# The scan stage of a hybrid vision block rebuilt: operands broadcast by DMA, decays in PSUM, products on GpSimd, directions added by an accumulating DMA

## The chip, the cores and the metric

The kernel runs on one core of a Trainium2 chip. The metric is the time of one execution in device microseconds (us), taken as the median of the runs shown; lower is better. A core has five engines with queues of their own: TensorE (PE in the profile, its weight loads PEld), VectorE (DVE), ScalarE (ACT), GpSimd (POOL) and SyncE (SP, which only issues DMAs here). Each engine works through its instructions in a fixed order. Where one waits, all that stand behind it on that engine wait too.

## The reference: what is computed

Four images of 64 x 64 tokens with 96 channels pass through a group norm and four layers. Layer 0 is a selective scan block over 192 inner channels, and it alone is changed:

```python
xz = x @ W_in.T
xp, z = xz[..., :192], xz[..., 192:]
xc = silu(conv3x3(xp) + conv_b)                  # u
xs = [xc by rows, xc by columns, and both reversed]   # four directions
dts, Bs, Cs = split(xs @ x_proj_w.T, [6, 16, 16])
delta = softplus(dts @ dt_proj_w.T + dt_proj_b)
# for each channel d (192) and state n (16), over the 4096 tokens t of a direction:
#   h[d, n] = exp(delta[t, d] * A[d, n]) * h[d, n] + delta[t, d] * u[t, d] * B[t, n]
#   y[t, d] = sum over n of h[d, n] * C[t, n]
y = sum of the four directions, each turned back to rows, + 4 * D * u
out = (y * silu(z)) @ W_out.T
```

The layers after it (a separable convolution, linear attention, two quantised feed-forward blocks and a spectral filter) are the same in both kernels.

## The kernel before, in words

`layer0` works on one image at a time, and `layers123` follows once all four images are through it. For image b, `pre(b)` makes, in eight blocks of 512 tokens, the gate `sz`, the convolved input `u`, the rows of B and C (`bc_s`), `delta_s` and `du_s` = delta times u; all of them go to DRAM. The scans then run over 24 groups (`NG`) of 8 channels: 8 channels x 16 states fill the 128 partitions. `post(b)` adds 4 D u, applies the gate, multiplies by `w_out` and stores x1.

For one group, `decay` (lines 237 to 255) loads 8 rows of delta and spreads each over its 16 states with a matmul against a 0/1 matrix `sel` (L248, tile `pa`). ScalarE then takes the exponential into `dA` (L252), 128 x 4096. `scan_group` (lines 257 to 322) spreads 8 rows of delta u in the same way (L275, `pb`), and VectorE multiplies them by the replicated B, `brep`, into `dB` (L279). ScalarE copies `dA` and `dB` into the column order (`dAT`, `dBT`, L281). Then VectorE runs four scans of 4096 steps: rows forward into `S` (L286), rows backward in place in `dB` (L287), columns forward into `T` (L294), columns backward in place in `dBT` (L295). It adds the two of each pair (L290, L298), adds the column sum to the row sum through a strided view (L299), and multiplies by the replicated C, `crep` (L307). TensorE sums the 16 states of each channel with the matrix `red` (L312, tile `py`), ScalarE copies the result out (L315), and SP stores it into `y_s` (L317).

`beside()` is called in the middle of a group. It gives out the next pieces of `post(b-1)` and `pre(b+1)`, and the `decay` of the next group. The tile framework's scheduler decides how these stand on each engine's queue. GpSimd issues stores in this stage and computes nothing in it. SP issues the loads and the stores of y. Before the first scan, `pre(0)` runs alone; after the last, `post(3)`. The lines named by the prediction are L236 (GpSimd's store of x1), L160, L179, L188, L207 (its other stores), L330 (the load of `brep`, one DMA for each 16 partitions), L491 and L666 (loads of the later layers) and L627 (a GpSimd memset there).

Of the kernel before, what the change touches and what calls it, by code (L numbers as in the profile page):

```python
# [10 lines left out]
F32 = mybir.dt.float32  # L11
# [7 lines left out]
NB = 4  # images  # L19
HW = 64  # rows, and columns, of an image  # L20
L = HW * HW  # tokens of an image
C = 96  # channels
DI = 192  # inner channels of the scan, and hidden ones of the spectral filter
NS = 16  # states of a scanned channel
NG = DI // 8  # groups of 8 scanned channels: 8 channels x 16 states on the partitions
RK = 6
BLK = 512  # tokens of one matmul: 8 image rows
# [3 lines left out]
N1 = 64  # the transform over 4096 tokens is 64 x 64  # L31


def conv_taps():
    """The 3x3 taps (ky, kx), the middle one first: it alone reaches every output."""
    return [(1, 1)] + [(y, x) for y in range(3) for x in range(3) if (y, x) != (1, 1)]


def tap_window(ky, kx, r0):
    """Rows (of the block's, from r0) and columns of the output that a tap reaches."""  # L40
    dy, dx = ky - 1, kx - 1
    ra, rb = max(0, -dy - r0), min(RPB, HW - dy - r0)
    ca, cb = max(0, -dx), min(HW, HW - dx)
    return dy, dx, ra, rb, ca, cb


@with_exitstack
def layer0(ctx: ExitStack, tc: tile.TileContext, a: dict, x1):
    """Group norm, the 2D selective scan block, the residual; x1[b] = relu(x + block), as the
    next layer reads it."""  # L50
# [20 lines left out]
    sel = const("sel", [40, 128], a["sel"])  # L71
# [3 lines left out]
    # Each of the four scans adds D u.  # L75
# [7 lines left out]
    delta_s = dram("delta_s", [DI, L])  # L83
    du_s = dram("du_s", [DI, L])
    bc_s = dram("bc_s", [2 * NS, L])
    u_s = dram("u_s", [DI, L])
    sz_s = dram("sz_s", [DI, L])
    y_s = dram("y_s", [DI, L])

    def halves(t):  # L90
        return t.rearrange("(c p) l -> p c l", p=C)
# [4 lines left out]
    def k4(name, shape=(C, 2, BLK)):  # L96
        return wk.tile(list(shape), F32, tag="k4", name=name, bufs=4)

    def pre_psum(name, rows=C, cols=BLK):
        t = ps.tile([128, BLK], F32, tag="pre", name=name, bufs=2)  # L100
        return t[:rows, :cols]

    def pre(b):
        """Everything before the scan, in blocks of 8 image rows."""
# [9 lines left out]
        # A group's three channels: its mean, and the mean of variance + squared distance of means.  # L114
# [15 lines left out]
        for i in range(NBLK):  # L130
# [4 lines left out]
            xb = k2("xb", (C, RPB + 2, HW))  # L135
# [3 lines left out]
            xn = k2("xn", (C, RPB + 2, HW))  # L139
            nc.scalar.activation(  # L140
                xn[:, :n, :], xb[:, :n, :], AF.Identity, scale=gn[:, 0:1], bias=gn[:, 1:2]
            )
            xp = k4("xp", (C, 2, RPB + 2, HW))
            for c in range(2):
                for ra, rb in ((0, 5), (5, n)):
                    p = pre_psum("p_xp", C, (rb - ra) * HW)
                    nc.tensor.matmul(
                        p, lhsT=w_in[:, c * C : (c + 1) * C], rhs=xn[:, ra:rb, :],
# [3 lines left out]
            sz = k4("sz")  # L152
            for c in range(2):
                p = pre_psum("p_z")
                nc.tensor.matmul(
                    p, lhsT=w_in[:, DI + c * C : DI + (c + 1) * C],
                    rhs=xn[:, r0 - lo : r0 - lo + RPB, :], start=True, stop=True,
                )
                nc.scalar.activation(sz[:, c, :], p, AF.Silu)  # L159
            nc.gpsimd.dma_start(halves(sz_s[b])[:, :, cols], sz)  # L160
            yield
            u = k4("u")
# [16 lines left out]
            nc.gpsimd.dma_start(halves(u_s[b])[:, :, cols], u)  # L179
# [8 lines left out]
            nc.gpsimd.dma_start(bc_s[b][:, cols], xd[RK : RK + 2 * NS, :])  # L188
            for c in range(2):
# [3 lines left out]
                # softplus(v) = max(v, 0) + log(1 + e), e = exp(-|v|); with w = fl(1 + e), the  # L193
                # logarithm is log(w) - ((w - 1) - e).
# [12 lines left out]
                nc.gpsimd.dma_start(delta_s[b][rows, cols], r)  # L207
                du = k2("du")
                nc.vector.tensor_tensor(du, r, u[:, c, :], ALU.mult)
                nc.gpsimd.dma_start(du_s[b][rows, cols], du)  # L210
            yield

    def post(b):
        """D u, the gate, the output projection and the residual."""
        for i in range(NBLK):
            cols = slice(i * BLK, (i + 1) * BLK)
            y, u, sz = k4("y_in"), k4("u_in"), k4("sz_in")
            nc.sync.dma_start(y, halves(y_s[b])[:, :, cols])
            nc.sync.dma_start(u, halves(u_s[b])[:, :, cols])
            nc.sync.dma_start(sz, halves(sz_s[b])[:, :, cols])  # L220
            xr = k2("xr")
            nc.sync.dma_start(xr, a["xT"][:, b * L + i * BLK : b * L + (i + 1) * BLK])
            p = pre_psum("p_out")
            for c in range(2):
                nc.vector.scalar_tensor_tensor(
                    y[:, c, :], u[:, c, :], d4[:, c : c + 1], y[:, c, :], ALU.mult, ALU.add
                )
            nc.vector.tensor_tensor(y, y, sz, ALU.mult)
            for c in range(2):
                nc.tensor.matmul(  # L230
                    p, lhsT=w_out[:, c, :], rhs=y[:, c, :], start=(c == 0), stop=(c == 1)
                )
            o = k2("o")
            nc.vector.tensor_tensor(o, p, xr, ALU.add)
            nc.scalar.activation(o, o, AF.Relu)
            nc.gpsimd.dma_start(x1[b][:, cols], o)  # L236
            yield

    def decay(b, g):
        """exp(delta A) of a group, [(channel, state), token]."""  # L240
        rows = slice(g * 8, (g + 1) * 8)
        dA = big.tile([128, L], F32, tag="dA", name="dA", bufs=2)
        for q in range(NBLK):
            if q % 2 == 0:
                dl = wk.tile([8, 2 * BLK], F32, tag="dl", name="dl", bufs=2)
                nc.sync.dma_start(dl, delta_s[b][rows, q * BLK : (q + 2) * BLK])
            pa = ps.tile([128, BLK], F32, tag="pa", name="pa", bufs=2)
            nc.tensor.matmul(  # L248
                pa, lhsT=sel[0:8, :], rhs=dl[:, (q % 2) * BLK : (q % 2 + 1) * BLK],
                start=True, stop=True,  # L250
            )
            nc.scalar.activation(  # L252
                dA[:, q * BLK : (q + 1) * BLK], pa, AF.Exp, scale=nega[:, g : g + 1]
            )
        return dA

    def scan_group(b, g, dA, brep, crep, beside):
        """The four scans of a group: by rows and by columns, each in both directions. They share
        their decays and inputs, and C is applied to the sum of their states."""
        rows = slice(g * 8, (g + 1) * 8)  # L260
        by_col = "p (w h) -> p h w"
        dAT = big.tile([128, L], F32, tag="dAT", name="dAT")
        dB = big.tile([128, L], F32, tag="dB", name="dB")
        dBT = big.tile([128, L], F32, tag="dBT", name="dBT")
        # The scans wait for these; the convolution beside them can come later.
        with tc.high_priority(offset=400):
            for q in range(NBLK):
                cols = slice(q * BLK, (q + 1) * BLK)
                hs = slice(q * RPB, (q + 1) * RPB)
                if q % 2 == 0:  # L270
                    # In another row group of the tensor engine than delta.
# [566 lines left out]
```

## Time and profile before

| | us |
|---|---|
| median of the 2 runs shown (9795.03 to 9818.39) | 9806.71 |
| span of the profiled execution, first to last instruction | 9822.7 |
| from the start to the load that precedes the first scan group | 482 |
| scans of the four images | 1742, 1736, 1785, 1667 |
| last `post` and `layers123` | some 2411 |
| VectorE busy in the whole span | 6735.3 |
| TensorE busy in the whole span | 6680.7 |
| ScalarE busy in the whole span | 3202.3 |
| GpSimd busy in the whole span | 159.9 |

The span is that of one profiled execution, and every duration below comes from it; it lies 16 us over the median. A row such as "L286 DVE TENSOR_TENSOR_SCAN S<-dA,dB 128x4096 ... x96 | 834.4, 8692" is read as: line 286, on VectorE, writes S from dA and dB, 96 times, 834.4 us in all and 8692 ns each. What stands behind the next bar is the idle time ahead of such instructions on their engine, and which instruction ended it.

### The profile page before, as it was taken

How to read it: one execution, taken by the hardware profiler on the slowest of the kernel's cores; microseconds unless marked ns; L12 is line 12 of the kernel's file. 1: busy time of each engine (PE TensorE's matmuls, PEld its weight loads, DVE VectorE, ACT ScalarE, POOL GpSimd, SP SyncE). 2: the span in 40 equal slices, each digit the busy share in tenths (PEclk: the TensorE clock that was granted, in tenths of full speed). 3: DMA queues.
4: the chain of work that ended last, by engine and by line, in shares of the span. 5: the costliest groups of instructions: out<-in, count | busy, mean ns of one | idle time of the engine just before them, and what ended most of it. 6: DMA issues, size and time to landing. Idle time of an engine off the chain costs nothing.

```text
span 9822.7 us, 58304 instructions
## 1 busy us (share of the span) xinstructions
PE 6680.7 (68%) x22202; PEld 3031.3 (31%) x22202; DVE 6735.3 (69%) x3526; ACT 3202.3 (33%) x4081; POOL 159.9 (2%) x296
## 2 busy tenths in 40 slices
PE   6767777754567666555666665554445888989888
PEld 2222222211122222111222211111112766848576
DVE  1188888887888888788988879989993323132232
ACT  3333434342334444333444433333330111121111
POOL 0000000000000000000000000000000000000000
PEclk8855565555566666555656655555556867777776
DMA  1110000002100000210000021000002010100000
GB/s 44 43 25 16 15 13 15 14 20 52 30 15 16 19 17 17 52 39 12 16 18 16 22 44 33 13 6 6 6 5 71 4 36 1 33 7 14 26 1 26
DMA packets 94661, 216.09 MB, mean 22 GB/s; under 512 B 25274, under 2 KB 26958, under 8 KB 92494
## 3 DMA queue, kind: packets, MB, share of 16 engines
q1 hardware_dynamic: 75950, 153.62, 6.4%
q0 software_dynamic: 18432, 58.74, 2.1%
q8 instruction: 177, 2.90, 0.1%
q14 instruction: 102, 0.84, 0.0%
HBM read 134.67 MB, written 77.59 MB: 22 GB/s over the span
## 4 chain that ended last, share of the span: by engine, by line
DVE 42%; PE 39%; ACT 8%; issue 8%; DMA 2%; SPq 0%; POOL 0%; DVEq 0%; ACTq 0%; POOLq 0%
DVE dB L287 8%; DVE T L294 8%; DVE dBT L295 6%; PE pb L275 6%; DVE S L286 6%; PE p_conv L169 5%; DVE S L290 4%; ACT dBT L281 4%; PE pa L248 4%; PE py L312 3%; PE p_l L499 3%; DVE S L299 2%; PE p_dft L653 2%; PE p_h L639 2%; ACT dAT L281 2%
## 5 line engine op out<-in xcount | busy, mean ns | idle before, releaser
L275 PE MATMUL pb<-du_g,sel 8*128 8x512 f32 x1536 | 1309.9, 1022 | 1517.7 <-DVE dB L279 1517.7
L248 PE MATMUL pa<-dl,sel 8*128 8x512 f32 x1536 | 1359.6, 1030 | 879.2 <-ACT dA L252 784.7
L281 ACT COPY dAT<-dA 128x512 f32<-128x512 f32 x768 | 772.3, 1104 | 2020.5 <-DVE dBT L295 2014.5
L286 DVE TENSOR_TENSOR_SCAN S<-dA,dB 128x4096 f32<-128x4096 f32 x96 | 834.4, 8692 | 576.2 <-PE py L312 494.2
L169 PE MATMUL p_conv<-xp,conv_w 96*96 96x504 f32 (+3 forms) x2304 | 1204.7, 684 | 2.8 <-ACT sz L159 2.8
L275 PEld LDWEIGHTS pb<-du_g,sel 8*128 8x128 f32 x1536 | 447.7, 307 | 2317.7 <-DVE dB L279 1843.4
L248 PEld LDWEIGHTS pa<-dl,sel 8*128 8x128 f32 x1536 | 411.2, 296 | 1762.8 <-ACT dA L252 1082.3
L287 DVE TENSOR_TENSOR_SCAN dB<-dA,dB 128x4096 f32<-128x4096 f32 x96 | 833.9, 8686 | 5.6 <-DVE S L286 0.5
L294 DVE TENSOR_TENSOR_SCAN T<-dAT,dBT 128x4096 f32<-128x4096 f32 x96 | 833.4, 8681 | 0.0
L295 DVE TENSOR_TENSOR_SCAN dBT<-dAT,dBT 128x4096 f32<-128x4096 f32 x96 | 833.2, 8679 | 0.1
L281 ACT COPY dBT<-dB 128x512 f32<-128x512 f32 x768 | 771.8, 1094 | 130.9 <-DVE T L298 80.8
L252 ACT ACTIVATE dA<-pa,nega 128x512 f32<-128x512 f32 x768 | 513.8, 685 | 715.2 <-PE pa L248 671.4
L299 DVE TENSOR_TENSOR S<-S,T 128x4096 f32<-128x4096 f32 x96 | 716.2, 7460 | 1.1
L169 PEld LDWEIGHTS p_conv<-xp,conv_w 96*96 96x96 f32 x2304 | 423.0, 190 | 802.8 <-issue 779.2
L279 DVE TENSOR_TENSOR dB<-pb,brep 128x512 f32<-128x512 f32 x768 | 492.9, 679 | 251.5 <-PE pb L275 201.8
L312 PE MATMUL py<-S,red 128*32 128x512 f32 x1536 | 401.7, 955 | 201.2 <-DVE S L307 177.3
L307 DVE TENSOR_TENSOR S<-S,crep 128x1024 f32<-128x1024 f32 x384 | 445.8, 1220 | 1.9
L290 DVE TENSOR_TENSOR S<-S,dB 128x4096 f32<-128x4096 f32 x96 | 424.4, 4421 | 2.0
L298 DVE TENSOR_TENSOR T<-T,dBT 128x4096 f32<-128x4096 f32 x96 | 423.9, 4416 | 0.3
L201 DVE TENSOR_SCALAR w<-e 96x512 f32<-96x512 f32 x64 | 26.3, 411 | 391.1 <-ACT e L199 391.1
L499 PE MATMUL p_l<-x,taps 96*96 96x504 f32 (+3 forms) x576 | 249.8, 597 | 29.8 <-DMA x<-x 29.8
L376 DVE COPY o<-p_o 128x192 f32<-128x192 f32 x64 | 22.9, 357 | 318.4 <-ACT o L372 318.4
(183 smaller groups left out, 6638.2 us busy)
## 6 DMA issues: line engine op xcount, KB each, us to landing
tw<-in_dft SPq DMA_DIRECT2D x32, 512.0 KB
sz_s<-sz POOLq DMA_DIRECT2D x32, 384.0 KB, 3.4
u_s<-u POOLq DMA_DIRECT2D x32, 384.0 KB, 3.4
delta_s<-r POOLq DMA_DIRECT2D x64, 192.0 KB, 2.4
du_s<-du POOLq DMA_DIRECT2D x64, 192.0 KB, 2.4
dl<-delta_s SPq DMA_DIRECT2D x384, 32.0 KB
du_g<-du_s SPq DMA_DIRECT2D x384, 32.0 KB
y_s<-ys SPq DMA_DIRECT2D x768, 16.0 KB
```

The lines of the kernel that those rows point to most:

```text
L169: nc.tensor.matmul(p[:, ra:rb, ca:cb], lhsT=conv_w[:, kc, ky * 3 + kx, oc * C : (oc + 1) * C], rhs=xp[:, kc, at + ra : at + rb, ca + dx : ...
L248: nc.tensor.matmul(pa, lhsT=sel[0:8, :], rhs=dl[:, (q % 2) * BLK : (q % 2 + 1) * BLK], start=True, stop=True,)
L275: nc.tensor.matmul(pb, lhsT=sel[32:40, :], rhs=du[32:40, (q % 2) * BLK : (q % 2 + 1) * BLK], start=True, stop=True,)
L281: nc.scalar.copy(dst.rearrange("p (w h) -> p w h", h=HW)[:, :, hs], src[:, cols].rearrange("p (h w) -> p w h", w=HW),)
L286: nc.vector.tensor_tensor_scan(S, dA, dB, 0.0, ALU.mult, ALU.add)
L287: nc.vector.tensor_tensor_scan(dB[:, ::-1], dA[:, ::-1], dB[:, ::-1], 0.0, ALU.mult, ALU.add)
L290: nc.vector.tensor_tensor(S, S, dB, ALU.add)
L294: nc.vector.tensor_tensor_scan(T, dAT, dBT, 0.0, ALU.mult, ALU.add)
L295: nc.vector.tensor_tensor_scan(dBT[:, ::-1], dAT[:, ::-1], dBT[:, ::-1], 0.0, ALU.mult, ALU.add)
L299: nc.vector.tensor_tensor(S.rearrange("p (h w) -> p h w", w=HW), S.rearrange("p (h w) -> p h w", w=HW), T.rearrange(by_col, h=HW), ALU.add,)
L312: nc.tensor.matmul(py[k : k + 32, :], lhsT=red, rhs=S[:, cols], start=True, stop=True)
L499: nc.tensor.matmul(p3[:, ra:rb, ca:cb], lhsT=taps[:, ky * 3 + kx, :], rhs=x3[:, r0 + dy + ra : r0 + dy + rb, ca + dx : cb + dx], start=(k ...
```

## The change

The row pair and the column pair of a group become two separate phases (b, g, o), o = 0 for rows and 1 for columns: 4 x 24 x 2 = 192 phases. A phase works in four steps q of 1024 tokens (`CH`).

- The partitions are ordered (state, channel), so one DMA can repeat 8 rows of delta, and of delta u, over all 128 partitions (`load`). No matmul spreads them.
- ScalarE takes the exponential from the loaded delta into PSUM (`decay`, tile `pa`, 128 x 1024, two buffers), once for the forward scan and once more for the backward one.
- GpSimd multiplies delta u by the replicated B (`inputs`) and the states by the replicated C.
- VectorE only scans, in steps of 1024: four forward, then four backward, each starting from the last column of the one before.
- The backward states are added to the forward ones by a DMA that accumulates, which GpSimd issues.
- The column order is made ahead in DRAM: `turn` loads a 96 x 4096 array, ScalarE copies it turned, and it is stored again, for B and C, delta, delta u, and for y of the columns in `post`.
- The stores of `pre` and `post` move from GpSimd's queue to SP's; work tiles have fewer buffers (`xp` one, `turn` and `turned` one).

Core of the diff (what is left out of `scan` and of the main loop is the same in kind):

```diff
+    def turn(src, dst):
+        n = src.shape[0]
+        t = wk.tile([C, L], F32, tag="turn", name="turn")
+        nc.sync.dma_start(t[:n, :], src)
+        for q in range(NCH):
+            o = wk.tile([C, CH], F32, tag="turned", name="turned")
+            w = CH // HW
+            nc.scalar.copy(
+                o[:n, :].rearrange("p (w h) -> p w h", h=HW),
+                t[:n, :].rearrange("p (h w) -> p w h", w=HW)[:, q * w : (q + 1) * w, :],
+            )
+            nc.sync.dma_start(dst[:, q * CH : (q + 1) * CH], o[:n, :])
...
+    def load(b, g, o):
+        rows = slice(g * 8, (g + 1) * 8)
+        dl, du = [], []
+        for q in range(NCH):
+            for dst, src, n, tag, bufs in ((dl, delta_s, "dl", "dl", 5), (du, du_s, "B", "B", 6)):
+                t = big.tile([128, CH], F32, tag=tag, name=n, bufs=bufs)
+                nc.sync.dma_start(
+                    t, src[o][b][rows, chunk(q)].unsqueeze(0).broadcast_to([NS, 8, CH])
+                )
+                dst.append(t)
+        return dl, du
+
+    def inputs(b, g, o, du):
+        for q in range(NCH):
+            nc.gpsimd.tensor_tensor(du[q], du[q], reps[o, 0][:, chunk(q)], ALU.mult)
+
+    def decay(g, dl, q):
+        pa = ps.tile([128, CH], F32, tag="pa", name="pa", bufs=2)
+        nc.scalar.activation(pa, dl[q], AF.Exp, scale=nega[:, g : g + 1])
+        return pa
+
+    def scan(b, g, o, dl, B, beside):
+        ...
+        for q in range(NCH):
+            pa = decay(g, dl, q)
+            s = big.tile([128, CH], F32, tag="S", name="S", bufs=6)
+            nc.vector.tensor_tensor_scan(
+                s, pa, B[q], S[-1][:, CH - 1 : CH] if S else 0.0, ALU.mult, ALU.add
+            )
+            S.append(s)
+        beside()
+        last = None
+        for q in reversed(range(NCH)):
+            pa = decay(g, dl, q)
+            nc.vector.tensor_tensor_scan(
+                B[q][:, ::-1], pa[:, ::-1], B[q][:, ::-1],
+                last[:, 0:1] if last is not None else 0.0, ALU.mult, ALU.add,
+            )
+            last = B[q]
+            nc.gpsimd.dma_start(S[q], B[q], accum_op=ALU.add)
+            nc.gpsimd.tensor_tensor(S[q], S[q], reps[o, 1][:, chunk(q)], ALU.mult)
+            if q % 2 == 1:
+                py = ps.tile([128, BLK], F32, tag="py", name="py")
+            for k in range(2):
+                at = 32 * (2 * (q % 2) + k)
+                nc.tensor.matmul(
+                    py[at : at + 32, :], lhsT=red, rhs=S[q][:, k * BLK : (k + 1) * BLK],
+                    start=True, stop=True,
+                )
+            if q % 2 == 0:
+                ys = wk.tile([128, BLK], F32, tag="ys", name="ys", bufs=2)
+                nc.scalar.copy(ys, py)
+                for j in range(4):
+                    i = 2 * q + j
+                    nc.sync.dma_start(
+                        y_s[o][b][rows, i * BLK : (i + 1) * BLK], ys[32 * j : 32 * j + 8, :]
+                    )
...
+        def beside():
+            nonlocal done
+            if nxt is not None:
+                if nxt[0] != b:
+                    replicas(nxt[0])
+                ahead.append(load(*nxt))
+                inputs(*nxt, ahead[0][1])
+            while done < min(n_aside, n_aside * (here + 1) // (2 * NG - 6)):
+                next(aside)
+                done += 1
```

## The prediction

> **What bounds the kernel now.** I read the chain that ended last first: VectorE holds 42% of it, TensorE 39%. Then the 40 slices and the stretches by image, to see where each holds.
>
> ```profile
> DVE 42%; PE 39%; ACT 8%; issue 8%; DMA 2%; SPq 0%; POOL 0%; DVEq 0%; ACTq 0%; POOLq 0%
> DVE  1188888887888888788988879989993323132232
> POOL 0000000000000000000000000000000000000000
> 482.00:2224.00 1742.00, 1207.80 (x1892) 373.92 (x1892) 1493.46 (x552) 705.26 (x835) 31.29 (x56) 0.58 0.07 17
> 5745.00:7412.00 1667.00, 814.78 (x1178) 241.59 (x1182) 1490.81 (x500) 539.93 (x629) 6.19 (x12) 0.50 0.07 16
> ```
>
> After the stretch the columns are its length and the busy us of PE, PEld, DVE, ACT and POOL, the granted TensorE clock, the DMA engines' share and GB/s. VectorE is busy for 86 to 89% of a scan stage and GpSimd is nearly idle; the DMA engines move 17 GB/s. So VectorE sets the pace from 482 to 7412 us. One undisturbed group on VectorE, from the timeline:
>
> ```profile
> 6490.10 8.69 DVE L286 TENSOR_TENSOR_SCAN S<-dA,dB 128x4096 f32<-128x4096 f32 x1 [4.26 <-PE py L312]
> 6507.62 4.42 DVE L290 TENSOR_TENSOR S<-S,dB 128x4096 f32<-128x4096 f32 x1
> 6540.53 7.64 DVE L299 TENSOR_TENSOR S<-S,T 128x4096 f32<-128x4096 f32 x1
> 6548.20 4.63 DVE L307 TENSOR_TENSOR S<-S,crep 128x1024 f32<-128x1024 f32 x4
> 6557.08 8.69 DVE L286 TENSOR_TENSOR_SCAN S<-dA,dB 128x4096 f32<-128x4096 f32 x1 [4.24 <-PE py L312]
> ```
>
> The period is 67.0 us, of which scans are 34.7. Four images take 6930; 96 x 67.0 is 6430, so the work of other images beside the scans costs 500.
>
> **Taken away, per group.** VectorE loses L279 (8 x 0.68 = 5.4 us), L290 and L298 (8.8), L299 (7.5) and L307 (4.9): 26.6 us. TensorE loses 16 `pa` and `pb` matmuls of some 1.0 us, ScalarE the 16 copies of 1.1 us at L281. These two only served VectorE.
>
> **VectorE after.** A plain two-input op takes 0.682 us for 512 (L206) and 4.42 for 4096 (L290): a constant of 0.15 us. Less that, a scan of 4096 (8.69) runs at 2.085 ns an element, and one of 1024 takes 2.28. With some 0.1 from one scan to the next (L287 starts 8.79 after L286) I take 2.35. That the decay comes from PSUM costs nothing: L279 reads PSUM at 679 ns for 512, L206, all from SBUF, takes 682. Eight scans are 18.8 us a phase, 37.6 a group against 67. This is VectorE's floor.
>
> **GpSimd after.** A phase gives it four B products (I0 to I3), four C products (T3 to T0) and four issues of an accumulating DMA (D3 to D0). No row shows an elementwise product or an accumulation. The nearest rows:
>
> ```profile
> L627 POOL MEMSET ln_s<- 1x4096 f32 x4 | 14.0, 3507 | 53.5 <-PE p_att L588 53.5
> L307 DVE TENSOR_TENSOR S<-S,crep 128x1024 f32<-128x1024 f32 x384 | 445.8, 1220 | 1.9
> L160 POOL DMA_DIRECT2D sz_s<-sz x32 | 21.5, 672 | 911.5 <-ACT sz L159 911.5
> sz_s<-sz POOLq DMA_DIRECT2D x32, 384.0 KB, 3.4
> delta_s<-r POOLq DMA_DIRECT2D x64, 192.0 KB, 2.4
> ```
>
> The memset gives GpSimd 0.856 ns an element for one stream. A product has two reads and a write: two streams' worth for 1024 is 1.75 us, three 2.63; VectorE's 1.22 is a far lower end. I take 2.2, the middle. An issue is 0.67. Landing grows by 1.0 us from 192 to 384 KB, so a plain 512 KB DMA lands after 4.1; if the second read doubles the part that grows with the data (2.7 of it), after 6.7. I take 5.4.
>
> The Trainium skill ("GPSIMD Engine Reference", section 3.1) gives 4497 ns for such an op at 2048 elements and advises VectorE for elementwise work; half of it, 2.25 us by estimate, would add 0.4 us a phase, 80 in all. The same skill ("Collectives: The Full Stack", part 3, why ReduceScatter is half of AllGather) puts an adding DMA at half the copy rate, since it reads two sources; that speaks for a landing of 6.7, with which the cycle below grows by 2.6 us and the total by 500. No run here shows either yet.
>
> **The cycle.** In the order in which the built kernel's instructions stand on GpSimd, a phase is most often D3 D2 D1 T3 T2 I0 T1 D0 I1 T0 I2 I3 (54 of 192); the I's are the next phase's, whose scans wait for them. Count from the start of the first backward scan. Those scans end at 2.35, 4.7, 7.05 and 9.4. D3, D2, D1 go out at the first three; T3 waits for D3's landing, 7.75 to 9.95; T2 waits until 10.1, to 12.3; I0 14.5, T1 16.7, D0 17.4 (its scan ended at 9.4: it stood behind four products), I1 19.6; T0 waits for D0's landing at 22.1, to 24.3; I2 26.5, I3 28.7. The last forward scan needs I3 and ends at 31.05, where the next backward scan starts. Where D0 stands ahead of T1 (D D D T T D T I T I I I) the same sum gives 28.9. I take 30 for all orders. With the low ends of both costs the first order gives 26.4, with the high ends 36.5; taking one off for the better orders, 25.5 to 35.
>
> So VectorE is idle for 11 of 30 us, and GpSimd's order is the bound: 20.3 us of its own work, the rest waits for landings. ScalarE needs 8 exponentials (L199: 0.63 us for 512, so at most 1.25 for 1024) and 1.2 us of copies, 11 us: it hides. SP's 16 issues a phase at 0.32 (four stores of y: 1.28) are 5 us; the stores moved to it from GpSimd add eight a block of `pre`, one a block of `post`. Each waits there for ScalarE's or VectorE's result, and behind it, as behind a waiting store of y, stand the loads for the phase ahead. They go out about a phase before they are needed; that slack is the cover, and a store held longer than it adds its excess to the cycle.
>
> **Transfers.** A phase loads 8 x 512 KB = 4.2 MB and accumulates 2.1 MB. Two stretches show what the DMA engines do when full:
>
> ```profile
> 474.00:476.00 2.00, 0.00 (x0) 0.00 (x0) 0.00 (x0) 0.00 (x0) 0.00 (x0) 0.50 1.13 131
> 7511.00:7512.00 1.00, 1.00 (x3) 0.41 (x2) 0.00 (x0) 0.00 (x0) 0.00 (x0) 0.50 1.04 422
> ```
>
> The first is the load of `brep`, 16 rows to 16 partitions a DMA; the second `tw`, 4 KB rows to 128 partitions. The new loads write 4 KB rows to 128 partitions but read the same 8 rows 16 times. Near the second, at 390 (7510 to 7513), they take 10.8 us a phase and the accumulations 5.4 to 10.8: hidden under 30.
>
> **Edges.** One `turn` loads 1.5 MB (the load at L491: 7.3 us on the chain) and, with one buffer, does four times a copy (2.2, twice L281) and a store to its landing (3.4): 30 us. Three stand ahead of the first column phase, one row phase hides 30 of their 90: 60 exposed. `post(3)` has two at the end: 60. Elsewhere 62 us of copies an image lie in ScalarE's idle time; if that cover is gone, 250 in all. Four replicas of 2 MB come anew at three borders: 45. The work beside the scans I keep at 500: its VectorE part fits the idle 11 us, but table loads (1283 ns each) and convolution waits now stand on ScalarE, between exponentials that the scans need at once; 100 to 900.
>
> **The sum**, on the profiled span of 9822.7: 482 (`pre(0)`, unchanged) + 2411 (behind the scans, unchanged) + 120 + 45 + 500 = 3558, plus 192 x period. At 30: 5760, in all 9318, less the 16 to the median: **9300**, 5% faster. A period of 32.6 us gives the time before.
>
> **Rivals.**
> 1. *The transfers set the pace* (slower). If repeated reads run like the `brep` stretch, at 131 GB/s, loads take 32 us and the accumulations at least 5.4 to 7: 39 us a phase, 11,050. For it: `brep` also fills many partitions from few rows. Against: each of its DMAs writes 16 partitions, the new ones all 128. It decides from about 190 GB/s downwards (4.2 MB in 22 us beside 10.8 of accumulation). Halfway, at 34 to 37 us, 10,100 to 10,650. Chance 0.27.
> 2. *Landings grow by contention to about 7 us*: the cycle's three waits bring it to 31.6 to 33.6; 9610 to 10,000, no change. Chance 0.14.
> 3. *GpSimd at its high ends* without full transfers: 35 us, 10,280. Chance 0.05.
> 4. *VectorE stays the bound*: products at 1.22 and landings at 2.7 give 21.3 us by the same cycle, 7650; down from the forecast's edge it covers 7650 to 8600. Nothing in the profile speaks for such products on GpSimd. Chance 0.09.
>
> The forecast, GpSimd's order as the bound at 26.3 to 31.6 us, 8600 to 9610, has 0.45. From these cases: faster by over 2% 0.54, within 2% (about what a measurement of this kernel can tell from no change) 0.14, slower 0.32. The range 8600 to 10,700 leaves out rival 4 and the worst of rival 1. That the change does not do what it says is hardly possible here: the built order shows products and accumulations on GpSimd.
>
> **What would show it.** GpSimd busiest in the stage and VectorE near 60%, waiting for B from GpSimd (the `inputs` line); GpSimd's own idle time ended by the accumulating DMA ahead of the C product; the product near 2.2 us; landings near 5.4; DMA share below 0.8. Wrong if VectorE or ScalarE waits for loaded `dl` or GpSimd for loaded `B` (rival 1), if a product is far from 2.2, or if ScalarE's exponentials, stuck behind convolution results, end VectorE's waits.

## The result and the profile after

The changed kernel takes 10700.91 us (median of 10697.41 and 10704.41). Before, it took 9806.71. The ratio is 1.091, with a 95% interval of 1.087 to 1.094: slower by 9%, where 5% faster was forecast. The profiled execution spans 10695.6 us.

First the page of the changed kernel: slices of VectorE, GpSimd and the DMA engines; then the DMA queues with packets, MB and their time as a share of 16 engines' span (q1 holds loads and stores, q0 the accumulations); then the groups that answer to L286, L299 and L307 of before; last the accumulation with its size and its median time to landing.

```profile
DVE  1254555444555554455555444455554322323232
...
POOL 0155555455555554445555445555555000000000
...
DMA  2577877787877778888777788787787200010100
...
q1 hardware_dynamic: 353724, 1114.23, 41.1%
q0 software_dynamic: 110592, 402.70, 19.6%
...
L311 POOL TENSOR_TENSOR S<-S,rep 128x1024 f32<-128x1024 f32 x768 | 1828.0, 2385 | 1455.4 <-DMA S<-B 1351.1
...
L283 POOL TENSOR_TENSOR B<-B,rep 128x1024 f32<-128x1024 f32 x768 | 1833.9, 2400 | 911.8 <-DMA rep<-bc_s 396.9
L297 DVE TENSOR_TENSOR_SCAN S<-pa,S,B 128x1024 f32<-128x1024 f32 x576 | 1352.9, 2349 | 1619.8 <-POOL B L283 1521.4
...
L297 DVE TENSOR_TENSOR_SCAN S<-pa,B 128x1024 f32<-128x1024 f32 x192 | 439.6, 2289 | 2097.2 <-POOL B L283 1939.6
L310 POOL DMA_DIRECT2D S<-B x768 | 673.7, 891 | 1655.1 <-DVE B L305 1408.7
...
S<-B POOLq DMA_DIRECT2D x768, 512.0 KB, 8.4
```

VectorE, at 8 and 9 tenths before, is at 4 and 5. No engine took its place: GpSimd is busy for 4238 of the 7863 us from 400 to 8263 us, VectorE for 3966, half of them. The DMA engines rose from under 1 tenth to 7 and 8. VectorE's forward scans wait for the B product, the C products wait for the accumulation. The chain of work that ended last is of no use here: its shares come to some 20% of the span, all in the layers behind the scans. So I read the waits instead, in us in total, times and longest. The last three lines are SP's own.

```profile
DVE S L297 <- POOL B L283: 3461.1, 517, 44.7
...
POOL S L311 <- DMA S<-B: 1351.1, 481, 12.7
...
SPq L274 <- DMA S<-B: 1506.3, 276, 12.4
SPq L326 <- ACT ys L323: 1482.0, 231, 18.8
SPq L117 <- ACT turned L113: 858.5, 107, 29.8
```

SP stood for 1506 us before loads that needed a buffer from an accumulation, and 2340 before stores of `ys` and `turned`, with loads behind them.

**One phase.** The timeline of the changed kernel, an undisturbed phase of the last image: start, length, engine, line; in brackets the idle time before it and what ended it. The VectorE lines are the backward scans that bound the phase, then come GpSimd's and SP's lines.

```profile
6504.14 9.61 DVE L305 TENSOR_TENSOR_SCAN B<-pa,B 128x1024 f32<-128x1024 f32 x4
...
6539.96 7.17 DVE L305 TENSOR_TENSOR_SCAN B<-pa,B 128x1024 f32<-128x1024 f32 x3
...
6507.01 0.87 POOL L310 DMA_DIRECT2D S<-B  x1 [5.53 <-DVE B L305]
...
6516.38 4.80 POOL L311 TENSOR_TENSOR S<-S,rep 128x1024 f32<-128x1024 f32 x2 [3.93 <-DMA S<-B]
6521.14 2.34 POOL L283 TENSOR_TENSOR B<-B,rep 128x1024 f32<-128x1024 f32 x1
6523.44 2.34 POOL L311 TENSOR_TENSOR S<-S,rep 128x1024 f32<-128x1024 f32 x1
6525.73 0.86 POOL L310 DMA_DIRECT2D S<-B  x1
6526.34 2.63 POOL L283 TENSOR_TENSOR B<-B,rep 128x1024 f32<-128x1024 f32 x1
6530.36 2.34 POOL L311 TENSOR_TENSOR S<-S,rep 128x1024 f32<-128x1024 f32 x1 [1.40 <-DMA S<-B]
6532.66 4.64 POOL L283 TENSOR_TENSOR B<-B,rep 128x1024 f32<-128x1024 f32 x2
...
6505.22 0.51 SPq L274 DMA_DIRECT2D dl<-deltaT_s  x1
6516.45 0.52 SPq L274 DMA_DIRECT2D B<-duT_s  x1
...
6523.82 12.79 SPq L326 DMA_DIRECT2D y_s<-ys  x8
6536.66 0.52 SPq L274 DMA_DIRECT2D dl<-delta_s  x1
```

GpSimd works off exactly the order that the prediction wrote down, D3 D2 D1 T3 T2 I0 T1 D0 I1 T0 I2 I3 (D an accumulation, T a C product, I a B product of the next phase). But T3 starts 9.4 us after D3 was issued, where 5.4 was taken. Stretches of the same phase show why (length, busy us of PE, PEld, DVE, ACT, POOL, granted clock, DMA share, GB/s):

```profile
6504.00:6508.00 4.00, 0.00 (x0) 0.00 (x0) 3.82 (x3) 2.24 (x2) 0.87 (x1) 0.50 1.02 235
...
6512.00:6516.00 4.00, 0.00 (x0) 0.00 (x0) 1.75 (x1) 1.58 (x2) 0.46 (x1) 0.50 1.06 218
...
6528.00:6532.00 4.00, 0.00 (x0) 0.00 (x0) 2.35 (x1) 0.00 (x0) 2.60 (x2) 0.50 0.45 84
6532.00:6536.00 4.00, 1.92 (x4) 0.19 (x4) 0.96 (x1) 1.27 (x2) 4.00 (x3) 0.50 0.00 0
```

Over a phase the DMA engines have time to spare, but not when it counts. D3 goes out when five loads of 512 KB have just been issued (6500.8 to 6505.2), and the engines are full until 6528, at 212 to 253 GB/s. Then they run empty, because SP stands before the stores of y until 6536.6. D0 is issued at 6525.73, while the last loads run out, and T0, which waits for it, starts 4.6 us later: the same 512 KB in the same phase in half of D3's time. Over all 768 accumulations the trace gives, from issue to landing:

```profile
DMA to landing us min/median/max: 4.5/8.4/37.1
```

The least, 4.5 us, lies below the 5.4 that the prediction took, the median far above it.

**Where 1377 us came from.** Take a phase as the distance between two first forward scans on VectorE's timeline (191 distances). Their median in the last image, where most phases have no other work, is 36.1 us; the mean over all is 41.0.

| term | forecast | measured | difference |
|---|---|---|---|
| `pre(0)` to the scans | 482 | 400 | -82 |
| 192 plain phases | 192 x 30 | 192 x 36.1 | +1171 |
| first column phase (`turn`) | 60 | 97.5 - 36.1 = 61 | +1 |
| three image borders (replicas) | 45 | 70.4 + 69.7 + 70.7 - 3 x 36.1 = 102 | +57 |
| other work beside the scans | 500 | 769, what is left of the stage | +269 |
| behind the last scan | 2411 + 60 | 2432 | -39 |
| sum | 9318 | 10,696 | +1377 |

### The profile page after: what moved, and what is told of

It reads as the page before. It is cut to its first block, busy times and chain, and to the rows that moved or that the text cites. A ratio compares the mean times of both kernels' runs of the same rounds, so it can differ in the third digit from the quotient of the medians.

```text
span 10695.6 us, 62297 instructions
## 1 busy us (share of the span) xinstructions
PE 4994.5 (47%) x20666; PEld 2226.8 (21%) x20666; DVE 4707.1 (44%) x3334; ACT 3227.9 (30%) x3666; POOL 4259.0 (40%) x2344
## 5 line engine op out<-in xcount | busy, mean ns | idle before, releaser
L317 PE MATMUL py<-S,red 128*32 128x512 f32 x3072 | 1338.6, 1000 | 4469.1 <-POOL S L311 4466.5
L311 POOL TENSOR_TENSOR S<-S,rep 128x1024 f32<-128x1024 f32 x768 | 1828.0, 2385 | 1455.4 <-DMA S<-B 1351.1
L287 ACT ACTIVATE pa<-dl,nega 128x1024 f32<-128x1024 f32 x1536 | 1713.0, 1117 | 2027.2 <-DVE S L297 873.7
L283 POOL TENSOR_TENSOR B<-B,rep 128x1024 f32<-128x1024 f32 x768 | 1833.9, 2400 | 911.8 <-DMA rep<-bc_s 396.9
L297 DVE TENSOR_TENSOR_SCAN S<-pa,S,B 128x1024 f32<-128x1024 f32 x576 | 1352.9, 2349 | 1619.8 <-POOL B L283 1521.4
L305 DVE TENSOR_TENSOR_SCAN B<-pa,B 128x1024 f32<-128x1024 f32 x768 | 1791.2, 2332 | 79.1 <-ACT pa L287 23.0
L297 DVE TENSOR_TENSOR_SCAN S<-pa,B 128x1024 f32<-128x1024 f32 x192 | 439.6, 2289 | 2097.2 <-POOL B L283 1939.6
L310 POOL DMA_DIRECT2D S<-B x768 | 673.7, 891 | 1655.1 <-DVE B L305 1408.7
L256 PE MATMUL p_out<-y_in,w_out 96*96 96x512 f32 x128 | 129.4, 1114 | 589.2 <-DVE y_in L255 589.2
L677 PE MATMUL p_dft<-dft,hb 128*64 128x64 f32 x3072 | 227.3, 315 | 9.4 <-DVE hb L667 9.4
L677 PEld LDWEIGHTS p_dft<-dft,hb 128*64 128x64 f32 x3072 | 225.7, 251 | 11.1 <-DVE hb L667 11.1
L556 PE MATMUL p_rstd<-ident,rs 128*96 128x128 f32 x1024 | 179.8, 358 | 27.8 <-DVE rs L551 27.8
```

The lines of the kernel that those rows point to most:

```text
L283: nc.gpsimd.tensor_tensor(du[q], du[q], reps[o, 0][:, chunk(q)], ALU.mult)
L287: nc.scalar.activation(pa, dl[q], AF.Exp, scale=nega[:, g : g + 1])
L297: nc.vector.tensor_tensor_scan(s, pa, B[q], S[-1][:, CH - 1 : CH] if S else 0.0, ALU.mult, ALU.add)
L305: nc.vector.tensor_tensor_scan(B[q][:, ::-1], pa[:, ::-1], B[q][:, ::-1], last[:, 0:1] if last is not None else 0.0, ALU.mult, ALU.add,)
L310: nc.gpsimd.dma_start(S[q], B[q], accum_op=ALU.add)
L311: nc.gpsimd.tensor_tensor(S[q], S[q], reps[o, 1][:, chunk(q)], ALU.mult)
```

## The experiments

My theory after this profile: the transfers do not fill the stage by their sum, but loads issued in a bunch on SP's queue fill the engines just when GpSimd waits for a landing. The rivals: the engines' time as such, however it is spread; the accumulation itself; and the loads' place behind waiting stores. In the table the plain phase is the median of the last image, as above, and the work beside is 191 times (mean less plain phase), edges included. The first eight changes were timed once each, the last four four times.

One thing limits what these runs can say: the scheduler plans GpSimd's order anew for each kernel. I compared the traces phase by phase, as sequences of D, T and I from one D3 to the next. The plain copy has the changed kernel's order in all 192 phases, and the loads of 128 different rows in 171. In the other kernels that issue four transfers a phase from GpSimd it is the same in 37 phases at most, and in those without such transfers it cannot be the same. So the first two experiments change one thing each, the second nearly; all others change the order as well, and their differences are not prices of the edit alone.

| kernel | us | plain phase | work beside |
|---|---|---|---|
| changed kernel | 10,701 | 36.1 | 935 |
| plain copy for the accumulation | 10,200 | 33.6 | 906 |
| loads of 128 different rows | 10,244 | 34.0 | 879 |
| delta loads of 64 tokens | 9248 | 26.0 | 1374 |
| delta loaded once | 8884 | 27.1 | 831 |
| y stores from ScalarE | 10,048 | 34.9 | 481 |
| no accumulation | 9701 | 30.1 | 1076 |
| accumulation of 64 tokens | 10,415 | 37.3 | 433 |
| both of 64 tokens | 9275 | 29.7 | 740 |
| addition on VectorE | 9260 | 28.1 | 1014 |
| ... and delta shared | 8764 | 29.0 | 349 |
| ... and y stores from ScalarE | 8596 | 27.8 | 401 |
| the same with the accumulating DMA | 9567 | 32.5 | 477 |

### A plain copy in the place of the accumulation

```diff
-            nc.gpsimd.dma_start(S[q], B[q], accum_op=ALU.add)
+            nc.gpsimd.dma_start(S[q], B[q])
```

The copy overwrites the forward states, so they are missing from the output.

> The accumulating DMA is replaced by a plain copy of the backward states over the forward ones (the forward direction is left out of the result); GpSimd's order stays nearly the same. In the changed kernel the accumulation lands after 8.4 us (median), takes 2.7 us of all 16 DMA engines (19.6% of the span for 768) and an undisturbed phase lasts 36 us. If the second read is what makes the landing long, the engines' time for one copy falls to 1.3 to 1.6 us, the landing to 6 or less, the phase to 33 or less and the time to 10,000 or less. If the loads beside it make it long, the landing stays at 7.5 or more, the phase at 35 or more and the time at 10,400 or more.

Measured: 10,200 us. The page of this kernel, with queue, issue and landing of the copy:

```profile
q0 software_dynamic: 110592, 402.70, 11.2%
...
L310 POOL DMA_DIRECT2D S<-B x768 | 431.1, 562 | 1765.9 <-DVE B L305 1566.8
...
S<-B POOLq DMA_DIRECT2D x768, 512.0 KB, 6.3
```

A copy takes 0.112 x 10,198.6 / 768 = 1.49 us of all 16 engines, an accumulation 0.196 x 10,695.6 / 768 = 2.73. The landing falls from 8.4 to 6.3 us, the issue from 0.89 to 0.56, and the plain phase from 36.1 to 33.6, with the same order on GpSimd. So adding instead of copying costs 500 us. The engines' time is what the first expectation said; landing, phase and time lie between the two. Even the plain copy lands at 6.3 us, above the 5.4 that I had taken for the adding one, so the second read is not all of it.

### The same loads from 128 different rows

```diff
-                    t, src[o][b][rows, chunk(q)].unsqueeze(0).broadcast_to([NS, 8, CH])
+                    t, src[o][b][0:128, chunk(q)]
```

Each load brings 128 different rows instead of 8 rows sixteen times, so the values are not the reference's.

> Each load takes 128 different rows of delta and of delta u in place of 8 rows 16 times over (so the scans run on the wrong channels): the same bytes, the same partitions. If reading the same rows 16 times slows the loads (212 to 253 GB/s with the DMA engines full, against 422 for the load of the transform's table), the DMA share of the stage falls by a fifth or more, the landing to 6.5 and the phase to 33 or 34, the time to some 10,200. If not, share, landing and time stay within 2%.

Measured: 10,244 us. The loads' queue and the accumulation on the page of this kernel:

```profile
q1 hardware_dynamic: 353724, 1114.23, 34.1%
...
S<-B POOLq DMA_DIRECT2D x768, 512.0 KB, 6.8
```

The same bytes take 0.341 x 10,242.1 = 3493 us of the engines; in the changed kernel they took 0.411 x 10,695.6 = 4396. That is 319 against 253 GB/s for the queue as a whole, in which these loads are 805 of the 1114 MB. Reading the same rows sixteen times does slow the loads, by 0.59 us each if the whole difference is theirs (903 us over 1536 loads). It is worth 457 us, a part of the loss only, near the first expectation.

This is the cleanest evidence for my theory. The accumulations are untouched and GpSimd's order is nearly so; only the loads beside them occupy the engines for less time. Yet the landing falls from 8.4 to 6.8 us, GpSimd's wait for landings from 1351 to 971 in all, and the plain phase from 36.1 to 34.0. Its wait for loaded B falls by 107 us only.

### Fewer bytes of delta, with and without the waits

In one kernel delta was loaded for the first phase only and then read again and again; in the other every load stayed where it was, but brought 64 tokens in place of 1024. Both outputs differ from the reference's by that.

```diff
+            if q not in fixed:
+                fixed[q] = big.tile([128, CH], F32, tag=f"dl{q}", name="dl", bufs=1)
+                nc.sync.dma_start(
+                    fixed[q], delta_s[o][b][rows, chunk(q)].unsqueeze(0).broadcast_to([NS, 8, CH])
+                )
+            dl.append(fixed[q])
```

> The rows of delta are loaded once, in the first phase, and all phases use them (so the decays of all other phases are not theirs); 2.1 of the 4.2 MB that a phase loads go away, nothing else. If the loads, which fill the DMA engines together with the accumulations (share 0.98 to 1.07 for 24 us on end in an undisturbed phase), make the landing long, it falls from 8.4 to about 5.5, the phase from 36 to 32 or 33, and the time to about 10,000. If the accumulation is slow by itself, the landing stays above 7.5 and the time above 10,400.

```diff
+                w = 64 if n == "dl" else CH
+                t = big.tile([128, w], F32, tag=tag, name=n, bufs=bufs)
...
-        nc.scalar.activation(pa, dl[q], AF.Exp, scale=nega[:, g : g + 1])
+        nc.scalar.activation(
+            pa.rearrange("p (a w) -> p a w", w=64),
+            dl[q].unsqueeze(1).broadcast_to([128, 16, 64]), AF.Exp, scale=nega[:, g : g + 1]
+        )
```

> Each delta load brings 64 tokens instead of 1024 (32 KB instead of 512), and the exponential reads them sixteen times over, so that its output is no longer the reference's; every load, wait and buffer stays where it was on SP. Theory 'bytes': 2.0 of the 4.2 MB that a phase loads are gone, as in the kernel that loaded delta only once (8,884), and the time is 8,850-9,150. Theory 'order on SP' (what that kernel won was that no load waited for a delta buffer): the waits are all still there, and the time stays over 10,200.

Measured: 8884 us with delta loaded once, far below both of its expectations, and 9248 with small loads (98 over what the bytes were to give). Two lines of the page of the kernel with small loads:

```profile
q1 hardware_dynamic: 353724, 736.74, 30.4%
...
S<-B POOLq DMA_DIRECT2D x768, 512.0 KB, 6.0
```

The accumulation is untouched, and lands at 6.0 us instead of 8.4. The plain phase falls by 10 us, to 26.0, more than the landings explain; that the loads of B come earlier too is likely, but not shown by itself. Of the 1817 us that loading delta once won, the small loads win 1453. The other 364 are not in the plain phase, which is longer with delta loaded once (27.1), but in the work beside it (831 against 1374); the loads of delta that still stand on SP in front of those of B may be the reason. GpSimd has the changed kernel's order in only 37 and 28 phases of these two kernels, so neither figure is a price.

### The stores of y from ScalarE's queue

```diff
-                    nc.sync.dma_start(
+                    nc.scalar.dma_start(
                         y_s[o][b][rows, i * BLK : (i + 1) * BLK], ys[32 * j : 32 * j + 8, :]
```

> The eight y stores of a phase (line 326) are issued by ScalarE, which has just made ys, and no longer by SP, where the next loads stood behind them (one store was held 12.8 us in the undisturbed phase, and the transfer engines lay idle for some 8 us of 36). The bytes stay the same. Theory 'order on SP': the loads go out earlier, the bunch of loads and accumulations is spread out, a phase falls from 36 to 30-33 us, and the whole to 9,600-10,100 us. Theory 'bytes': the engines have the same work and the accumulations the same neighbours, the gain is under 200 us, 10,500-10,700.

Measured: 10,048 us, 653 less with the same bytes. But the plain phase falls by 1.2 us only, to 34.9, not to 30-33: the landing stays at 8.5 us, and SP now waits at the next place. Its waits and GpSimd's in this kernel:

```profile
SPq L274 <- DMA S<-B: 3494.4, 658, 14.2
...
POOL S L311 <- DMA S<-B: 1923.5, 613, 15.8
```

SP's wait for B's buffers, which the accumulations hold until they land, grew from 1506 to 3494 us, and VectorE's wait for exponentials from 180 to 1176. Most of what the edit won, 454 of 653 us, is in the work beside the scans: 481 instead of 935. The loads and stores of `pre`, `post` and `turn` stand on the same queue as the scans' loads, and each store there waits for an engine. But only 3 of the 192 phases kept GpSimd's order, so what the stores' place alone is worth is not shown.

### Leaving the accumulation out, or most of its bytes

Three kernels were to price the accumulation alone. The first leaves it out:

```diff
-            nc.gpsimd.dma_start(S[q], B[q], accum_op=ALU.add)
```

> The accumulation and its issue are left out, so the backward states are missing from the output; the loads, products, scans and stores stay. Theory 'GpSimd's cycle with its landings': GpSimd has eight products of 2.35 us a phase, VectorE eight scans of 2.35, so a phase takes 20-24 us with the work beside the scans, and the whole 7,600-8,300. Theory 'order and bytes of the loads' (the loads alone set the pace): 4.2 MB a phase at the 247-253 GB/s that the loads had so far is 17 us and hidden by the scans; only if the loads are late for their place on SP does a phase stay over 28 us, 8,900 or more.

Measured: 9701 us, with a plain phase of 30.1: the second expectation's number, but its reason, late loads, is only a part. The timeline of an undisturbed stretch, GpSimd and VectorE:

```profile
7109.74 2.34 POOL L310 TENSOR_TENSOR S<-S,rep 128x1024 f32<-128x1024 f32 x1 [2.53 <-DVE S L297]
7112.04 2.34 POOL L283 TENSOR_TENSOR B<-B,rep 128x1024 f32<-128x1024 f32 x1
...
7114.41 2.35 DVE L297 TENSOR_TENSOR_SCAN S<-pa,S,B 128x1024 f32<-128x1024 f32 x1 [4.82 <-POOL B L283]
```

Without the accumulation a C product needs no backward scan any more, and the scheduler put it (L310 here) between the B products. It waits for a forward scan to be through with `S`; the next B product stands behind it, and the next forward scan waits for that: 4.8 us idle, a step of 7.2 us instead of 2.4. The late loads are the other part: in the whole run GpSimd waits 1104 us for loaded B, 515 in the changed kernel. The run says nothing of the accumulation's price, since GpSimd's order moved with the edit.

The second adds 64 tokens of a chunk only (32 KB of 512), the third makes the delta loads small as well. The rest of the backward states is missing from both outputs.

```diff
-            nc.gpsimd.dma_start(S[q], B[q], accum_op=ALU.add)
+            nc.gpsimd.dma_start(S[q][:, :64], B[q][:, :64], accum_op=ALU.add)
```

> The accumulating DMA adds the first 64 tokens of a chunk alone (32 KB instead of 512), so most of the backward states are missing from the output; its issue, its landing and all that waits for it stay. Theory 'bytes on the transfer engines': the landing falls from 8.4 to 2-3 us, 8.6 us of all engines' time a phase are gone (4 x 2.73 less a little), and the time is 8,800-9,300 us. Theory 'latency and issue' (what counts is that GpSimd issues a DMA and waits for its end, of whatever size): 10,000 or more.

> Delta loads and accumulations of 64 tokens each, all waits, issues and buffers in place: the phase that is left is GpSimd's order, the scans and the B loads. Theory 'bytes': GpSimd has 8 x 2.35 + 4 x 0.9 = 22.4 us a phase and some 4 us of waits for scans and landings; with the work beside the scans the whole is 8,200-8,700 us, and the two together bring less than the sum of each alone. Theory 'order on SP and waits': over 9,000.

Measured: 10,415 and 9275 us, both as the second expectation had it. Against the kernels with the same loads and whole accumulations that is 286 less and 27 more. The last line of each page's part on DMA issues that concerns the accumulation, first with full, then with small delta loads:

```profile
S<-B POOLq DMA_DIRECT2D x768, 32.0 KB, 4.5
```

```profile
S<-B POOLq DMA_DIRECT2D x768, 32.0 KB, 2.7
```

The same small accumulation lands at 2.7 us where the delta loads are small, and at 4.5 where they are whole: the landing goes with the other traffic. In one phase of the second kernel an accumulation is issued 1.0 us after the last of three loads (7577.6 to 7579.4), and GpSimd's timeline shows when the C product that waits for it could start:

```profile
7579.86 0.88 POOL L310 DMA_DIRECT2D S<-B  x1
...
7587.15 2.33 POOL L311 TENSOR_TENSOR S<-S,rep 128x1024 f32<-128x1024 f32 x1 [3.20 <-DMA S<-B]
7589.46 2.33 POOL L283 TENSOR_TENSOR B<-B,rep 128x1024 f32<-128x1024 f32 x1
```

That is 7.3 us for 32 KB, about what three loads of 0.52 MB take at 243 GB/s, the rate of that stretch (6.5 us). Again GpSimd's order moved with the edit: here it is D3 D2 T3 D1 T2 D0 T1 I0 T0 I1 I2 I3, with the first B product 16.7 us behind D3 (7572.78), 14.1 in the changed kernel. So a phase takes 34 us at best and 37.3 in the median. What the accumulated bytes are worth at an unchanged order stays open.

### The addition on VectorE, shared delta, stores from ScalarE

Four kernels go the other way and mend what the profile shows. The first three are complete kernels; each has the edits of the one before.

```diff
-            nc.gpsimd.dma_start(S[q], B[q], accum_op=ALU.add)
+            nc.vector.tensor_tensor(S[q], S[q], B[q], ALU.add)
```

> The backward states are added by VectorE (four tensor_tensor of 1024, 1.22 us each, a phase) in place of the accumulating DMA. If GpSimd's order with its waits for landings sets the pace, both waits (9.4 and 4.6 us in an undisturbed phase) and the issues (0.86 each) go, VectorE needs 18.8 + 4.9 us, GpSimd 18.7, and the cycle gives 26 to 29 us a phase: 8700 to 9300, faster than both kernels. If the loads set the pace (4.2 MB at some 230 GB/s are 18 us), the same follows, as the accumulations' share of the DMA engines goes too. If VectorE's two-input adds and GpSimd's products hinder each other, products grow from 2.34 and adds from 1.22, and the phase comes to 31 or more: over 9700.

Measured: 9260 us, a ratio of 0.942 (0.940 to 0.944) to the kernel before, as the first two expectations had it; the run cannot tell them apart. The addition takes 1.27 us, 5.1 a phase. VectorE has the time, and the plain phase falls to 28.1 us. The work beside the scans stays at 1014. The third expectation is true in part: a GpSimd product that runs beside such an addition for over 1 us takes 3.35 us in the median (220 of them), one that runs beside none 2.34.

In the second, delta is loaded for the row order alone; the exponentials of the column order read the same tile turned. `deltaT_s` and its two `turn` calls go; S has 5 buffers, `u` one, the 2 KB work tiles 6.

```diff
+            if q == 0 and o == 0:
+                held[0] = big.tile([128, L], F32, tag="dl", name="dl", bufs=2)
...
+                dl.append(
+                    held[0].rearrange("p (h w) -> p w h", w=HW)[:, q * w : (q + 1) * w, :]
+                )
```

> VectorE adds the backward states in place of the accumulating DMA, and delta is loaded once for both orders of tokens: the second order's exponentials read the first order's rows with a stride of 64 tokens (there is no turned delta any more; S has 5 buffers, u 1, the 2 KB work tiles 6). Theory 'landings and bytes': no transfer that anyone waits for is left on GpSimd, and 3.1 MB are loaded a phase instead of 4.2; VectorE has 8 x 2.35 + 4 x 1.27 = 23.9 us a phase, the whole is 400 + 192 x (25 to 28) + 2,440, 7,650-8,250, plus up to 300 for the work beside the scans. Theory 'order on SP': the B loads still stand behind the y stores and now behind one delta tile of a whole row, and the time stays about 9,000-9,300, as it was with VectorE's addition alone.

Measured: 8764 us, ratio 0.894 (0.892 to 0.895), between the two expectations. Phases of 26.2 us are there, among others of 28 to 36; the median of 29.0 is no lower than before, and the gain is in the work beside, 349 instead of 1014. The exponential grew from 1.12 to 1.57 us on the mean, since those that read with a stride take 2.0.

The third adds the y stores from ScalarE (the diff is that of the stores above).

> The last kernel (VectorE's addition, delta loaded once for both orders) with the y stores issued by ScalarE. Theory 'order on SP': SP waited 1,465 us for ys ahead of stores with B loads behind them, GpSimd waited 240 us for B from memory; the time falls to 8,400-8,650 us. Theory 'VectorE and GpSimd by turns': undisturbed phases already run at 26 us, of which VectorE works 24, and the time stays within 8,700-8,820.

Measured: **8596 us**, ratio 0.877 (0.875 to 0.878), 12% faster than the kernel before, as the first expectation had it. Page of this kernel, VectorE's slices and two groups:

```profile
DVE  1278998889888888988888898888622231231322
...
L324 POOL TENSOR_TENSOR S<-S,rep 128x1024 f32<-128x1024 f32 x768 | 1835.2, 2390 | 1639.1 <-DVE S L323 1563.9
...
L323 DVE TENSOR_TENSOR S<-S,B 128x1024 f32<-128x1024 f32 x768 | 1015.6, 1322 | 15.2
```

VectorE is the bound again, busy for 5001 of the 5744 us from 400 to 6144. GpSimd's products wait for it; it waits itself for exponentials, 438 us ahead of the forward scans.

The fourth is this kernel with the accumulating DMA back in the place of VectorE's addition.

> The kernel of 8,596 us with the accumulating DMA back in the place of VectorE's addition: delta is loaded once for both orders, ScalarE issues the y stores. Theory 'bytes and order on SP are what went wrong, the accumulating DMA is only dear': 3.1 MB are loaded a phase in place of 4.2 and the accumulations land in 6 us, as where delta was loaded once (8,884), the stores no longer hold the loads, and the time is 8,550-8,850 us. Theory 'the accumulation itself': GpSimd still waits for each landing, a phase takes what it took there or more, and the time is 8,850-9,300.

Measured: 9567 us, ratio 0.975 (0.973 to 0.977). The accumulation costs 971 us against VectorE's addition, in surroundings where the loads are a quarter smaller and SP is clear of y stores. This is on the side of my second expectation, and 267 us over its upper end. The page of this kernel:

```profile
L324 POOL TENSOR_TENSOR S<-S,rep 128x1024 f32<-128x1024 f32 x768 | 1831.9, 2391 | 1312.3 <-DMA S<-B 1307.1
...
S<-B POOLq DMA_DIRECT2D x768, 512.0 KB, 7.0
```

GpSimd still waits 1307 us for landings of 7.0 us. Besides, an accumulation holds its S and B buffers until it lands: SP waits 4368 us for B's, and VectorE 672 for TensorE to be through with S, of which this kernel has 5 buffers and not 6. It is also slower than the kernel that loaded delta once (8884); that one had 6 buffers for S, loaded no delta at all and had another order on GpSimd, and I cannot split the 683 us among these.

## Why the prediction was wrong

**The cycle: right mechanism, one term mis-sized.** GpSimd's order is the bound of a plain phase, as forecast, VectorE waits for B and GpSimd for the accumulation ahead of T3 and T0. From the first backward scan on, the phase shown has T3 at 12.24 us (forecast 7.75) and the next phase at 35.82 (31.05). All but 0.3 of the 4.8 us between them stands ahead of T3: D3 is issued 0.5 later, and its landing takes 9.4 us, not 5.4. Behind T3 the chain took 23.6 us, forecast 23.3. The other term is a choice: I took 30 for all orders where the commonest one gave 31.05.

**The step that failed** is "Landing grows by 1.0 us from 192 to 384 KB [...] I take 5.4". It took median landings from a kernel that moved 17 GB/s and used them in one that moves 180. For an accumulation that little stands beside, 5.4 was even too much: the least is 4.5, and D0 took 4.6. Beside the loads it is 8.4 in the median, and 9.4 for the D3 shown. "Hidden under 30" was the other half of the step. The engines' time does fit: 4.2 MB of loads take 16.6 us of all engines at 253 GB/s (forecast 10.8 at 390), four accumulations 10.9 (forecast 5.4 to 10.8), together 27.5 us, less than a phase. But GpSimd waits for single transfers, and these land behind the bunch that SP has just issued. The two runs that kept GpSimd's order, wholly or nearly, bear this out from both sides: the landing falls from 8.4 to 6.8 us when only the loads beside it get quicker, and to 6.3 when the accumulation becomes a copy; the plain phase falls by 2.1 and 2.5 us, and of the 457 and 500 us won, GpSimd's waits for landings account for 380 and 414. With the order moved, 8.4 falls to 6.0 when delta's bytes go, and for 32 KB 4.5 falls to 2.7.

The warning was in the trace of before, under its medians. There the stores of `delta_s` (L207), 192 KB, land after 2.4 us in the median, the figure that the prediction used. From issue to landing:

```profile
DMA to landing us min/median/max: 2.3/2.4/15.4
```

The longest is that of the store issued at 467.85 us, right behind six loads of `brep` of 256 KB each.

**The work beside the scans** was put at 500 with 100 to 900 as its ends, and came to 769. The reason given there, table loads and convolutions on ScalarE, was probably not what counted most: VectorE waited 180 us in all for exponentials. The forecast did say that a store waiting on SP holds the loads behind it, and let the slack of a phase cover that. In the plain phase it seems to, almost: moving the y stores won 1.2 us a phase, though one was held for 12.8. Beside other work it seems not to: the same edit took 454 us off there. As GpSimd's order moved with that edit, both are likely and not shown.

**The borders** cost 34 us each, not 15: the reload of the replicas blocks the C and B products, with three waits of some 31 us for `rep<-bcT_s`. Its 8.4 MB alone are 21.5 us at the 390 GB/s that the prediction took elsewhere. `pre(0)` was 82 us shorter than before, where no change was forecast. TensorE is as busy in it, 340 and 344 us. But before, it also waited 54.5 us for ScalarE's `xn`, of which 1.9 are left, and 43.8 for `dl` ahead of the `pa` matmuls, which are gone. Why `xn` no longer holds it I have no run on.

**What held:** scans of 2.35 us a step (2.35 and 2.33), exponentials hidden (1.12 us each), the first `turn` 60 us (61), DMA share under 0.8 (0.79 in the stage), GpSimd the busiest engine there; VectorE was at 50%, where near 60 was named. A product was put at 2.2 us: 2.34 where nothing disturbs it, 2.39 on the mean, some 1.5 us a phase. The Trainium skill ("GPSIMD Engine Reference", section 3.1), from which 2.25 was estimated, is closer. What it says of an adding collective ("Collectives: The Full Stack", part 3), half the copy's rate, nearly holds here for the engines' time, 2.73 against 1.49 us.

**The rivals.** Rival 2, landings that grow by contention, was the mechanism, but priced at 7 us a landing and 10,000 at most. Rival 1 has the time, nearly (10,100 to 10,650 at half way), but not by its condition: the loads' queue runs at 253 GB/s, above the 190 at which the transfers were to set the pace, and the engines stand empty for some 6 of the 8 us from 6528 on. Its sign, waits for loaded operands, is there in part: ScalarE waits 488 us for `dl` and GpSimd 515 for B, against 1351 for landings. The two should have been one case: transfers need not fill the phase to be late in it.

## What to carry to other kernels

Where an engine's queue waits for a DMA's landing, price it with the traffic that the change itself puts in front of it; a median landing from a quiet trace is close to its lower end, and the longest landing there is worth a look. Loads that share a queue with stores that wait for results can go out late and in bunches, so try the two on different queues, and compare the sum of an added engine operation (5 us on an idle VectorE here) with the whole wait that a transfer adds, buffers held included. And when an edit changes what an instruction depends on, its queue or its length, compare the planned order before reading its time as a price: here it stayed in one of twelve runs, and nearly in one more.

## What the runs showed of the hardware

- With loads that read 8 rows sixteen times their queue runs at 253 GB/s here, with the same loads from 128 different rows at 319; other transfers are 28% of its bytes.
- An accumulation of 512 KB lands 4.5 us after its issue at the least, 8.4 in the median beside 4.2 MB of loads a phase, and 6.8 where the same loads take less of the engines' time.
- An accumulating DMA of 512 KB takes 2.73 us of all 16 engines and 0.89 us to issue on GpSimd; the plain copy takes 1.49 and 0.56.
- An accumulation of 32 KB, issued behind three loads of 512 KB, held the product that waited for it for 7.3 us; at the least such an accumulation lands in 2.1.
- A GpSimd product of 128 x 1024 takes 2.34 us, and 3.35 beside a VectorE addition from two SBUF tiles.
- ScalarE's exponential of 128 x 1024 takes 1.12 us from a dense tile and 2.0 from one read with a stride of 64 elements.
